# A four-image block on one core: projection with its taps stacked to 128 rows, a shorter split of the scan's rows, and all scans as one sequence beside projections 1 to 3

## The chip, the cores and the metric

The kernel runs on one core of one Trainium2 chip. The metric is device time in microseconds (us) from start to end, the median of several executions. Executions of one kernel on one chip agree within 0.3%. Engines in the profile: PE is TensorE (PEld its weight loads), DVE is VectorE, ACT is ScalarE, POOL is GpSimd, and SPq is the queue from which SyncE issues transfers.

## The reference, cut to what matters

The input is four images of 96 channels and 128 x 128 points. For each image:

```python
z = einsum('bchw,dc->bdhw', x, in_w) + in_b          # x normalised; 96 -> 192 channels
z = silu(depthwise_conv3x3(z, dw_w) + dw_b)           # "projection"
xs = stack([z, z.T, flip(z), flip(z.T)])              # 4 directions, 16384 points each
x_dbl = einsum('bkdl,ked->bkel', xs, x_proj_weight)   # 8 rows: 6 for delta, B, C
delta = softplus(einsum(dts_r, dt_projs_weight) + bias)
dA = exp(delta * A);  dBu = delta * B * xs
h[l] = dA[l] * h[l-1] + dBu[l]                        # the scan
y = h * C + D * xs                                    # the 4 directions are added up
... normalisation of y, product with out_w            # "norm"
... a second block: attention weights ("maps") from 3x3 convolutions, and their application
```

The second block is not changed. What is in front of it is: the projection, the split of the x_dbl rows into three bf16 pieces, and the order in which scans are run.

## The kernel before

A scan is cut into steps of 128 channels x 1024 points. Two images and six groups of channels make 384 steps. One step touches four engines:

```python
def deltas(n, half):        # TensorE "d": pd = wdt x rows; ScalarE: dl = softplus(pd)
def decays(n):              # ScalarE: dA = exp(A * dl), for two steps
def times_u(n):             # GpSimd: dl = dl * u
def spread(n, q):           # TensorE: pB or pC = row B or C on 128 channels
def times_b(n):             # VectorE: pB = dl * pB
def scan(n):                # VectorE: dA = scan(dA, pB)
def times_c(n):             # VectorE: dl = dA * pC
def into_y(n):              # GpSimd: y = y + dl

for n in range(total):      # the order in which the program is written
    spread(n, 1); scan(n)
    times_u(n + 1)
    if n: into_y(n - 1)
    if n % 2 == 0: deltas(n + 3, 0); deltas(n + 3, 1); decays(n + 2)
    yield 2.6
    times_c(n)
    spread(n + 1, 0); times_b(n + 1)
    if n % 2: deltas(n + 3, 0); deltas(n + 3, 1)
    if n % 2: u_in(n + 3)
    else: rows_in(n + 4)
    yield 2.6
```

The compiler has a scheduler that may move instructions within the bounds of their dependences; the order that it chose is fixed in the compiled program.

```python
def rows_in(n):             # split rows of two steps; one transfer of 60 rows for each image
    xr = p1.tile([KS, 2 * SN], BF16, name="xr", bufs=3)
    for a, img in enumerate(imgs):
        nc.sync.dma_start(xr[a * KI : (a + 1) * KI], xsp[img][k][:, sl])

for j in range(2):          # projection: 2 x 96 channels, 9 taps, 97 rows on the array
    for t in range(KK):
        nc.tensor.matmul(pz, lhsT=weff[:, t, j * C : (j + 1) * C],
            rhs=xs[:, q * R + dh : q * R + dh + R, dw : dw + W],
            start=(t == 0), stop=(t == KK - 1))
        if t % 3 == 2 and t < KK - 1: yield 2.6

drain(projections(0, weff, psl))                    # images 0 and 1, no scans
co_run(projections(1, weff, psl), scans, 0.9)       # images 2 and 3, beside the scans of 0 and 1
drain(scans)
co_run(imgs[0].norm(...), last, 0.8)                # scans of 2 and 3 beside image 0's norm and maps
co_run(imgs[0].attend(psl), last, 1.0)
```

co_run interleaves two programs by the numbers that they yield.

## Time and profile before

| | before |
|---|---|
| median | 9351.4 us (3 runs, 9351.3 to 9352.1) |
| TensorE busy, granted clock | 84% of the span, 0.91 |
| a scan step beside the maps | 7.8 us (1070 us, 137 steps in the compiled order) |
| a scan step's work on GpSimd, ScalarE, VectorE | 5.4, 5.0, 4.8 us |

How to read it: a step needs no engine for more than 5.4 us.

### The profile page before, as it was taken

To read this page: it belongs to the slowest core of one execution; us is meant where nothing else is said; L and a number is where in the kernel's file an instruction comes from. 1 tells how busy PE (TensorE), PEld (TensorE's weight loads), DVE (VectorE), ACT (ScalarE), POOL (GpSimd) and SP (SyncE) were. 2 spreads that over 40 slices of the span, in tenths; PEclk is the share of its full clock that TensorE was granted. 3 is DMA by queue.
4 is the path that set the end of the run, shared out by engine and by line. 5 is a ranking of instruction groups with operands and counts; after the bars stand their busy time and mean duration, and the time that the engine had idled before them with its cause. 6 is when DMAs were issued, how large, how long until landed. Compare 5 with 4: busy or idle time off the path is not lost. (4 is left out here: it accounts for less than half of the span.)

```text
span 9352.3 us, 86318 instructions
## 1 busy us (share of the span) xinstructions
PE 7879.3 (84%) x31732; PEld 4127.8 (44%) x31732; DVE 3474.7 (37%) x3463; ACT 3293.0 (35%) x3977; POOL 2188.9 (23%) x1153
## 2 busy tenths in 40 slices
PE   5993993999399948199999929997999989899997
PEld 1331331333032312066665306565656667467763
DVE  1004004267556448637675343322023331130003
ACT  0004003288378547648674141232111241111111
POOL 1003003267447436338684000000000000000000
PEclk9995996999589968599999969998999999999998
DMA  2115114144633345865555678448376474673237
GB/s 67 43 34 128 39 36 120 57 154 133 153 116 114 120 122 164 174 172 175 168 150 164 183 176 199 133 133 168 94 185 159 117 172 110 151 182 85 73 97 197
DMA packets 832687, 1220.49 MB, mean 131 GB/s; under 512 B 141225, under 2 KB 639906, under 8 KB 819977
## 3 DMA queue, kind: packets, MB, share of 16 engines
q1 hardware_dynamic: 830248, 1214.75, 49.7%
q8 instruction: 252, 4.13, 0.2%
q14 instruction: 171, 1.39, 0.1%
q0 software_dynamic: 2016, 0.22, 0.0%
HBM read 869.16 MB, written 345.01 MB: 130 GB/s over the span
## 5 line engine op out<-in xcount | busy, mean ns | idle before, releaser
L352 PE MATMUL bank<-xs,weff 97*96 97x512 f32 x4608 | 2088.5, 605 | 4.7 <-DVE xs L318 2.6
L352 PEld LDWEIGHTS bank<-xs,weff 97*96 97x96 f32 x4608 | 737.9, 165 | 1235.7 <-issue 1216.5
L577 POOL TENSOR_TENSOR y<-y,dl 128x1024 f32<-128x1024 f32 x384 | 1055.3, 2748 | 816.3 <-DVE dl L571 754.4
L551 POOL TENSOR_TENSOR dl<-dl,u 128x1024 f32<-128x1024 f32 x384 | 1011.3, 2643 | 607.1 <-ACT dA L522 292.1
L983 POOL MEMSET vt<- 96x9 f32 x60 | 6.7, 111 | 3345.1 <-DMA vd<-vt 2648.0
L702 PE MATMUL bank<-y,w_v 128*96 128x384 f32 (+1 forms) x2064 | 714.9, 494 | 76.9 <-DMA y<-x1d 69.8
L702 PE MATMUL bank<-y,w_c 128*96 128x384 f32 (+1 forms) x2064 | 706.0, 488 | 58.7 <-ACT half L945 30.9
L555 DVE TENSOR_TENSOR pB<-dl,pB 128x1024 f32<-128x1024 f32 x384 | 470.3, 1225 | 667.3 <-PE pB L532 360.5
L725 PEld LDWEIGHTS bank<-w_k,y 128*128 128x128 f32 x3360 | 659.6, 261 | 40.4 <-issue 31.1
L725 PEld LDWEIGHTS bank<-w_q,y 128*128 128x128 f32 x3360 | 658.4, 260 | 41.9 <-issue 29.3
L725 PE MATMUL bank<-w_q,y 128*128 128x96 f32 (+2 forms) x3360 | 667.8, 352 | 1.6 <-ACT cc L1003 1.6
L725 PE MATMUL bank<-w_k,y 128*128 128x96 f32 (+2 forms) x3360 | 665.8, 352 | 0.0
L361 ACT ACTIVATE zt<-bank,dwb 96x512 f32<-96x512 f32 x256 | 175.0, 683 | 1355.3 <-PE bank L352 1354.5
L532 PE MATMUL pB<-xr,wbc 60*128 60x512 bf16 (+1 forms) x768 | 270.1, 431 | 416.5 <-DVE dA L568 248.0
L1090 PE MATMUL bank<-v,wat 128*32 128x384 f32 (+1 forms) x6336 | 531.2, 481 | 50.0 <-DMA watr<-watd 33.3
L513 PE MATMUL pd<-xr,wdt 60*128 60x512 bf16 (+1 forms) x768 | 276.6, 428 | 320.2 <-DMA xr<-xsp 270.0
L425 ACT ACTIVATE dl<-pd,dtb 128x512 f32<-128x512 f32 x768 | 491.5, 684 | 123.4 <-PE pd L513 102.6
L425 ACT ACT_TABLE_LOAD x328 | 420.8, 1283 | 311.4 <-PE pd L513 306.5
L532 PEld LDWEIGHTS <-wbc 60*128 60x128 bf16 (+1 forms) x1536 | 127.5, 102 | 909.7 <-issue 323.4
L702 PEld LDWEIGHTS bank<-y,w_v 128*96 128x96 f32 x2064 | 334.8, 165 | 415.0 <-issue 388.3
L571 DVE TENSOR_TENSOR dl<-dA,pC 128x1024 f32<-128x1024 f32 x384 | 466.9, 1216 | 134.7 <-PE pC L532 113.9
L702 PEld LDWEIGHTS bank<-y,w_c 128*96 128x96 f32 x2064 | 331.6, 163 | 383.5 <-issue 345.0
(202 smaller groups left out, 8838.7 us busy)
## 6 DMA issues: line engine op xcount, KB each, us to landing
u<-zb SPq DMA_DIRECT2D x192, 1024.0 KB
xr<-xsp SPq DMA_DIRECT2D x256, 240.0 KB
zb<-zt SPq DMA_DIRECT2D x128, 384.0 KB
yms<-y SPq DMA_DIRECT2D x96, 512.0 KB
yc<-yms SPq DMA_DIRECT2D x128, 384.0 KB
y<-x1d SPq DMA_DIRECT2D x336, 97.0 KB
y<-x2d SPq DMA_DIRECT2D x336, 97.0 KB
v<-vd SPq DMA_DIRECT2D x160, 193.6 KB
```

Of the source, the lines that this page charges most:

```text
L352: nc.tensor.matmul(pz, lhsT=weff[:, t, j * C : (j + 1) * C], rhs=xs[:, q * R + dh : q * R + dh + R, dw : dw + W], start=(t == 0), stop=(t ...
L361: nc.scalar.activation(zt[:, j, :, q * R : (q + 1) * R].rearrange("p b h w -> p h b w"), pz.rearrange("p h (b w) -> p h b w", w=UW), AF.Si ...
L425: nc.scalar.activation(dst, src, AF.Softplus, bias=bias)
L513: nc.tensor.matmul(pd, lhsT=wdt[0 : xr.shape[0], g, k], rhs=xr[:, at : at + CH], start=True, stop=True,)
L532: nc.tensor.matmul(p[:, j : j + CH], lhsT=wbc[0 : xr.shape[0], steps[n][0], q], rhs=xr[:, at + j : at + j + CH], start=True, stop=True,)
L551: nc.gpsimd.tensor_mul(t, t, u_view(n))
L555: nc.vector.tensor_mul(p, live[n]["dl"], p)
L571: nc.vector.tensor_mul(live[n]["dl"], live[n]["dA"], live[n]["C"])
L577: nc.gpsimd.tensor_add(v, v, t.rearrange("p (a b) -> p a b", b=W))
L702: nc.tensor.matmul(pc[:, :n], lhsT=w, rhs=y[:, 0:n, o : o + W], start=(at == 0), stop=(at == len(terms) - 1),)
L725: nc.tensor.matmul(pk[:, k0 * C : k1 * C], lhsT=y[:, kh, sw : sw + 382 : 3], rhs=w.rearrange("p t o -> p (t o)"), start=(i == 0), stop=(i ...
L1090: nc.tensor.matmul(pc[p : p + 32].rearrange("p (a b) -> p a b", b=W), lhsT=(wr if k == 2 else ws[k][:, d])[:, c : c + 32], rhs=y, start=(n ...
```

## The change

Three parts. (1) The projection puts channel-and-tap pieces of 128 rows on the array, so that 7 terms take the place of 9, for 128 output channels; the last 64 channels of two row chunks share the array's columns as two tiles. (2) The split works on two pieces in place of four and stores its rows once, in place of three times; the scan's load rebuilds the three copies, with four transfers per image in place of one. (3) All 384 steps are one sequence that starts beside projection 1.

```diff
-                            nc.tensor.matmul(pz, lhsT=weff[:, t, j * C : (j + 1) * C], ...)   # 9 taps, 2 x 96
+                    terms = [(k, d) for d in range(3) for k in range(2)] + [(2, 0)]
+                        jobs = [(0, 128, 0, q)] if q < 2 else [(0, 64, 128, 0), (64, 128, 128, 1)]
+                            nc.tensor.matmul(pz[p:e]..., lhsT=ws[k][:, d, c : c + e - p], rhs=window(ys[k], at, d, n), ...)
 ...
-            for f in range(4):          # split: rows stored three times
+            for f in range(2):          # stored once, as xdt and xbc
 ...
-                    nc.sync.dma_start(xr[a * KI : (a + 1) * KI], xsp[img][k][:, sl])
+                    src = xdt[img][k % 2, k // 2].rearrange("i r l -> (i r) l")[:, sl]
+                    for w in range(3):
+                        nc.sync.dma_start(xr[at + 18 * w : at + 18 * w + 18], src)
+                    src = xbc[img][k % 2, k // 2].rearrange("i r l -> (i r) l")[:, sl]
+                    nc.sync.dma_start(xr[at + 54 : at + KI], src)
 ...
-        for p in range(npair):
-            scans = ssm_scan(zb[p], xsp[p], yms[p])
-            ... co_run(projections(p + 1, weff, psl), scans, 0.9)
+    last = ssm_scan(zb, xdt, xbc, yms, ready)
+        drain(projections([0], weights, psl))
+        co_run(projections(range(1, NB), weights, psl), last, 1.35)
-    co_run(imgs[0].norm(yms[0][0], psl, "left"), last, 0.8)
-    co_run(imgs[0].attend(psl), last, 1.0)
+    co_run(imgs[0].norm(yms[0][0], psl, "left"), last, 1.0)
+    co_run(imgs[0].attend(psl), last, 0.6)
```

A step's own instructions are the same in both kernels.

## The prediction

> **What bounds the kernel now.** I read the page's first two parts for the regimes, then the costliest groups, then the windows view with one window per stage, then the waits of a few windows. The groups give the main actors:
>
> ```profile
> L352 PE MATMUL bank<-xs,weff 97*96 97x512 f32 x4608 | 2088.5, 605 | 4.7 <-DVE xs L318 2.6
> L577 POOL TENSOR_TENSOR y<-y,dl 128x1024 f32<-128x1024 f32 x384 | 1055.3, 2748 | 816.3 <-DVE dl L571 754.4
> L551 POOL TENSOR_TENSOR dl<-dl,u 128x1024 f32<-128x1024 f32 x384 | 1011.3, 2643 | 607.1 <-ACT dA L522 292.1
> L425 ACT ACT_TABLE_LOAD x328 | 420.8, 1283 | 311.4 <-PE pd L513 306.5
> L522 ACT ACT_TABLE_LOAD x322 | 413.1, 1283 | 5.7
> ```
>
> L352 is the projection: 4608 passes, two for each of 2304 fp32 matmuls. L577 and L551 show 384 scan steps. A step costs GpSimd 2.75 + 2.64 = 5.4 us; VectorE 1.23 + 1.22 + 2.35 (scan) = 4.8 us; ScalarE 2 x 0.684 + 1.146 + 0.28 (first passes) + 650/384 loads x 1.283 = 5.0 us. No engine could do 384 steps in less than about 2070 us; the program spends 750 to 5060 us on them. The windows, cut where the counts of L352, L571 and L763 change, show why (columns: window, length, busy of PE, PEld, DVE, ACT, POOL, then granted clock, DMA share, GB/s):
>
> ```profile
> core 0: us, PE busy (x) PEld busy (x) DVE busy (x) ACT busy (x) POOL busy (x), PEclk, DMA share, GB/s
> 117.00:668.00 551.00, 551.00 (x1256) 193.81 (x1257) 46.70 (x45) 48.59 (x68) 18.16 (x29) 1.00 0.15 42
> 668.00:884.00 216.00, 55.35 (x119) 13.95 (x117) 99.42 (x94) 89.98 (x96) 66.98 (x33) 0.54 0.53 128
> 884.00:1445.00 561.00, 558.74 (x1276) 196.40 (x1277) 55.39 (x51) 48.73 (x69) 26.41 (x33) 0.99 0.15 40
> 1445.00:1680.00 235.00, 79.07 (x169) 20.79 (x168) 136.53 (x112) 102.25 (x107) 121.22 (x45) 0.54 0.52 135
> 1680.00:2335.00 655.00, 644.69 (x1632) 219.27 (x1631) 350.19 (x240) 427.79 (x437) 354.89 (x156) 0.99 0.37 115
> 2335.00:2555.00 220.00, 54.90 (x117) 13.55 (x116) 128.86 (x109) 83.09 (x90) 107.07 (x42) 0.53 0.58 144
> 2555.00:3290.00 735.00, 716.78 (x1726) 225.97 (x1726) 401.12 (x272) 486.98 (x497) 409.91 (x179) 0.96 0.37 119
> 3290.00:3420.00 130.00, 20.73 (x45) 4.91 (x44) 46.15 (x32) 46.74 (x49) 33.84 (x14) 0.52 0.51 113
> 3420.00:3990.00 570.00, 314.18 (x679) 95.74 (x677) 418.00 (x396) 399.44 (x443) 270.38 (x126) 0.70 0.65 165
> 3990.00:5090.00 1100.00, 1060.84 (x4482) 707.03 (x4483) 694.66 (x500) 721.38 (x835) 726.92 (x290) 0.97 0.57 167
> ```
>
> Read in order: projection 0, split, projection 1, split, 2, split, 3, split, normalisation of image 0, its attention maps. The projections and maps are bound by TensorE (97 to 100% busy, clock near 1). The four splits are not: TensorE is a quarter busy and the others half. What follows 5090 us (4262 us) does not contain a changed instruction; it is TensorE's as well.
>
> What holds the splits shows in the waits of the first:
>
> ```profile
> POOL dl L551 <- issue: 169.9, 3, 165.9
> PE pd L513 <- DMA xr<-xsp: 104.8, 4, 84.8
> DVE t L403 <- DMA t<-xrow: 39.3, 1, 39.3
> ACT piece L190 <- DMA t<-xrow: 35.0, 2, 34.7
> ```
>
> The scan waits for split rows, and these for a queue of issues. The timeline of the queue gives: 16 column loads 32 us, 96 stores of the first half to 758 us, 96 of the second to 799 us, only then the next image's 16 statistics loads, and projection 1 at 884. In the second split, GpSimd's memset of xs waits 55.2 us for the stores of the pieces: the next projection reuses the split's memory.
>
> **What the Trainium skill says.** "TensorEngine Tiling (Array Packing)", section Tiling Modes: independent tiles of the array run matmuls in parallel; two for outputs up to 64 columns. The trace has the case of four tiles: 1662 passes of L1090 (mostly 384 columns, 32 outputs) took 140.5 us in the chain, 85 ns each, where L352's rate, 435 ns for 512 columns (below), gives 326 ns for a lone pass of 384. It agrees: four ran in the time of one. "Perfetto Trace Analysis", section Identifying the Most-Contended Engine: matmul busy time is no measure of throughput. It agrees: L352's mean is 605 ns, but 574 passes start in the 250 us from 1000 on, 435 ns each, which I use. "TensorE: Matmul & The Clock Gate", Part 1: after idling the array runs at half clock. Agrees: 0.53 in the splits. "ScalarE: Activation LUTs", section What ACT_TABLE_LOAD costs: 1283 ns and a drain of some 1380 ns. The trace has the 1283 ns, but the next ACTIVATE follows at once, so I charge 1.283.
>
> **The change, part by part.**
>
> *Projection.* Before, an image needs 16 strips x 36 matmuls, plus 4 x 16 of L328, at 2 x 0.435 us: 576 x 0.87 + 64 x 0.87 = 557 us (window 1: 551). After, a strip has 7 terms for each of two chunks of 128 channels, and 7 pairs for the remaining 64 channels of both chunks side by side on the columns: 21 slots. The row product has four matmuls in two concurrent pairs: 2 slots. 16 x 23 x 0.87 = 320 us. The gain is 237 us of TensorE per image. Added per strip: seven copies of about 1 MB within the chip, on the DMA queues. That is about 2.5 MB a strip with loads and stores, 125 GB/s over 20 us; windows here reach 260, so I take it as hidden when alone.
>
> *Split.* 192 stores of 7.9 MB become 24 of 3.1 MB; the scan's reads rebuild the triplicate. Column loads stay at 32 us. Each of two halves: load 4, copy 2, three casts 2, two subtractions 2.4: about 17 us, one after the other as there is one buffer; landing 5. 32 + 34 + 5 = 71 us instead of 120. Then statistics, 84 us before with 15 steps beside them; with 9 I take 70. A gap of 140 to 150 instead of 216 to 235; the last, without statistics, 100 instead of 130.
>
> *One sequence of scans.* I counted steps between markers in TensorE's instruction order of the two built programs, where the order is fixed:
>
> before: 14 in split 0, 0 beside projection 1, 20, 64 beside 2, 20, 74 beside 3, 7, 48 in norm, 137 in maps.
> after: 9 in split 0, 54 beside projection 1, 6, 76 beside 2, 20, 76 beside 3, 13, 50 in norm, 80 in maps.
>
> A step's six matmuls cost TensorE: (645 + 717 - 2 x 557)/138 = 1.8 us beside projections; (1061 - 703)/137 = 2.6 us in maps, where 703 us is an image's 3136 passes of maps at the 224 ns that 8500 to 9000 us shows.
>
> - Start: 117 to 138 us, my estimate: more weight pieces, the border rows made through memory, a stack to copy before the first matmul.
> - Projection 0 alone: 320 (551).
> - Gap: 140 (216).
> - Projection 1: 320 + 54 x 1.8 = 417, at 96%: 435 (561).
> - Gap: 140 (235).
> - Projections 2 and 3: 320 + 76 x 1.8 = 457 on TensorE. ScalarE: the order has 301 table loads in steps 96 to 256, so 76 x (1.37 + 1.15 + 0.28 + 2.41) + 48 x 0.68 + casts = 440. VectorE 76 x 4.8 + 45 = 410, GpSimd 410. Four engines at 88% or more cannot mesh perfectly; I take 525 each (655 and 735).
> - Gaps: 150 and 100 (220, 130).
> - Norm: 570, with the same steps.
> - Maps: 703 + 80 x 2.6 = 911, at 97 to 98%: 930 (1100).
> - The rest: 4262.
>
> Sum: 138 + 320 + 140 + 435 + 140 + 525 + 150 + 525 + 100 + 570 + 930 + 4262 = **8235 us**, 12% less.
>
> **The rivals.** *The pairs do not overlap.* Then 7 more slots a strip: 6.1 x 64 = 390 us of TensorE, of which nearly all lies on the path: about 8600. Against it: L1090. *The stack starves TensorE.* Normalising, copying and multiplying form a chain through GpSimd, VectorE and the in-order DMA queue, where scan loads that wait for buffers stand in front. 5 us late in each of 48 strips is 240 us: 8470. For it: DMA would rise from 115 to some 180 GB/s beside projections (a strip's 2.5 MB and 4.75 steps' 3.1 MB in 31 us). Against: a whole bank group, some 13 us, lies between copy and use. *The other engines become the bound.* GpSimd, ScalarE and VectorE at 7.5 us a step, as slow as the best stage beside projections before, add 2 x 45 us: 8325. In the other direction, 6.3 us a step, which 39 to 40 steps in 4250 to 4500 show, gives 8140. *The gain stays hidden.* If the scans were the only bound, faster projections would change nothing. The windows speak against it: GpSimd is 54 to 66% busy until 5090.
>
> **Range and chances.** Gaps may be off by 30 us each, the two full stages by 60 each, maps and start by 60: together about 150, with more room on the slow side for starvation. 8040 to 8440. Within 2% would need 950 us of the gain to vanish.
>
> **What would show it.** Projection 0 alone at 20 us a strip, with pairs starting within tens of ns; if 26, the overlap failed. Between projections, gaps near 140 us with 24 stores. Projections 2 and 3 at 6.9 us a step, TensorE near 88%; if waits of TensorE for y0, y1 or y2 exceed 50 us in sum, the stack starves it. Maps starting near 3045 and ending near 3975. After that, the same 4262 us within 20; if it is not, I have overlooked something in the tail.

## More of the kernel before

In the page of the kernel before, two lines of the 40 slices (tenths of busy time of TensorE, and its granted clock) show the short dips of the splits and little else, and one group shows VectorE's product with B (columns: busy, mean ns of one; idle time in front of it, what ended most of it) waiting for TensorE more than for GpSimd:

```profile
PE   5993993999399948199999929997999989899997
PEclk9995996999589968599999969998999999999998
L555 DVE TENSOR_TENSOR pB<-dl,pB 128x1024 f32<-128x1024 f32 x384 | 470.3, 1225 | 667.3 <-PE pB L532 360.5
```

## The result, and the profile after

The changed kernel takes 9747.8 us (median of 4 runs, 9738.9 to 9751.1) and the kernel before 9351.7 in the same rounds (9351.3 to 9361.5). The ratio is 1.0419, with a 95% interval of 1.0401 to 1.0437. Ratios here are the mean time of one kernel's runs over that of the other's in the same rounds, so not quite the ratio of the medians. The chips of the five groups of runs below gave the kernel before medians from 9352 to 9408 us, so I compare ratios throughout.

It is **4.2% slower**, where 12% faster was predicted. The same lines of the page after, the slices and the groups of the projection and of the scan:

```profile
PE   5846645566376646528999983998989998999997
PEclk9967777777577767758999996999999999999998
L431 PE MATMUL bank<-y,wp 128*128 128x512 f32 (+3 forms) x3584 | 1357.4, 628 | 37.7 <-DMA y<-y 25.3
L670 POOL TENSOR_TENSOR y<-y,dl 128x1024 f32<-128x1024 f32 x384 | 1060.9, 2763 | 1460.8 <-DVE dl L664 1339.1
L648 DVE TENSOR_TENSOR pB<-dl,pB 128x1024 f32<-128x1024 f32 x384 | 470.7, 1226 | 1687.0 <-POOL dl L644 1413.1
```

After projection 0 TensorE is half idle for 16 slices, and its clock falls to 0.7. The projection itself is as cheap as hoped (1357 us of busy time against 2088), and it waits only 38 us for its stack. What grew are the scan's waits: VectorE's product with B waits 1413 us for GpSimd (before, GpSimd was not its main releaser), and GpSimd's addition waits 1339 us for VectorE (754 before). The windows view of four stages (projection 0, 2, 3, and the maps; columns as in the prediction: window, length, busy of PE, PEld, DVE, ACT, POOL, then clock, DMA share, GB/s):

```profile
100.00:440.00 340.00, 331.66 (x1028) 119.41 (x1028) 29.52 (x40) 38.88 (x54) 2.12 (x29) 1.00 0.47 123
1530.00:2420.00 890.00, 564.17 (x1476) 173.44 (x1476) 388.36 (x259) 434.74 (x452) 402.19 (x182) 0.74 0.40 117
2650.00:3520.00 870.00, 598.26 (x1474) 171.52 (x1476) 386.91 (x259) 418.22 (x438) 416.64 (x182) 0.73 0.39 112
4400.00:5470.00 1070.00, 999.63 (x4092) 666.13 (x4091) 419.73 (x315) 432.42 (x539) 415.45 (x174) 0.94 0.43 121
```

Projection 0 alone takes 340 us, where 320 were predicted. Beside projections 2 and 3 no engine is over 70% busy. That is a loop of waits, and the timeline of the changed kernel shows it (start, duration, engine, line, operation; in brackets the idle time in front and its releaser). One turn, from an addition into y to the next:

```profile
2198.82 2.34 POOL L670 TENSOR_TENSOR y<-y,dl 128x1024 f32<-128x1024 f32 x1 [5.18 <-DVE dl L664]
2201.12 2.34 POOL L644 TENSOR_TENSOR dl<-dl,u 128x1024 f32<-128x1024 f32 x1
2203.49 1.23 DVE L648 TENSOR_TENSOR pB<-dl,pB 128x1024 f32<-128x1024 f32 x1 [4.82 <-POOL dl L644]
2204.82 2.35 DVE L661 TENSOR_TENSOR_SCAN dA<-dA,pB 128x1024 f32<-128x1024 f32 x1
2207.27 1.22 DVE L664 TENSOR_TENSOR dl<-dA,pC 128x1024 f32<-128x1024 f32 x1
2208.64 2.34 POOL L670 TENSOR_TENSOR y<-y,dl 128x1024 f32<-128x1024 f32 x1 [5.18 <-DVE dl L664]
```

The product with u at 2201 waits in GpSimd's queue behind the addition of an earlier step, which waits for VectorE; VectorE then waits for that product. Five instructions in a ring take 9.8 us. Their data do not ask for this ring: by the same timeline ScalarE was through with the product's dl at 2196.3, 4.8 us before the product began. (The product's u came in the same load as that of the step before, whose product ran at 2191.3.) It is the order of GpSimd's queue.

That order can be read from the compiled program without a chip. I counted, at each step's spread of C, how many further steps of deltas TensorE has already issued ("TensorE's lead"), and at each addition into y how many further products with u GpSimd has issued ("GpSimd's lead"), as a mean over the 384 steps. Before: 1.79 and 1.27. After: **0.37 and 0.41**. The order of start times in the traces gives the same numbers. TensorE's order also changed in a second way. Its list, near step 40 of the kernel before and step 180 of the changed one, both beside a projection (d: deltas, B and C: spreads, P: projection matmuls, here with those of the row product; with how many in a row):

```
before  P3 B2 d2 P5 C2 d2 P3 B2 P3 C2 P3 B2 d2 P3 C2 d2 P3 B2 P2 C2 d2 ...
after   C2 P18 d2 B2 C2 P4 d2 P9 B2 C2 d4 B2 C2 B2 C2 d2 B2 C2 d2 P4 B2 P3 C2 P22 d2 ...
```

Before, at most five projection matmuls stand in front of the scan's next in this stretch; after, up to 22. An fp32 matmul is two passes of 435 ns, and a run may hold pairs that go side by side; a run of that kind, timed below, took 17.6 us.

### The profile page after: what moved, and what is told of

Read it like the earlier page. It is cut to its first block, busy times and chain, and to the rows that moved or that the text cites. A ratio compares the mean times of both kernels' runs of the same rounds, so it can differ in the third digit from the quotient of the medians. Undisturbed runs are those within 1.5% of the kernel's fastest.

```text
span 9737.1 us, 85329 instructions
## 1 busy us (share of the span) xinstructions
PE 7348.7 (75%) x30708; PEld 3869.2 (40%) x30708; DVE 3377.1 (35%) x3387; ACT 3159.6 (32%) x3820; POOL 2121.1 (22%) x1161
## 5 line engine op out<-in xcount | busy, mean ns | idle before, releaser
L431 PE MATMUL bank<-y,wp 128*128 128x512 f32 (+3 forms) x3584 | 1357.4, 628 | 37.7 <-DMA y<-y 25.3
L625 PE MATMUL pB<-xr,wbc 60*128 60x512 bf16 (+1 forms) x768 | 325.3, 509 | 1278.7 <-DVE dA L661 641.1
L431 PEld LDWEIGHTS bank<-y,wp 128*128 128x128 f32 (+3 forms) x3584 | 479.3, 172 | 827.4 <-issue 778.5
L504 ACT ACT_TABLE_LOAD x306 | 392.6, 1283 | 820.9 <-PE pd L606 818.1
L606 PE MATMUL pd<-xr,wdt 60*128 60x512 bf16 (+1 forms) x768 | 337.9, 505 | 355.9 <-DMA xr<-xbc 287.8
L1099 DVE BATCH_NORM_STATS2 c2st<-cc 96x6 f32<-96x384 f32 (+1 forms) x172 | 94.8, 552 | 1144.0 <-ACT cc L1098 1143.4
```

What stands on the lines that cost most here:

```text
L431: nc.tensor.matmul(pz[p:e].rearrange("p (h w) -> p h w", w=W), lhsT=ws[k][:, d, c : c + e - p], rhs=window(ys[k], at, d, n), start=(i == 0 ...
L504: nc.scalar.activation(dst, src, AF.Softplus, bias=bias)
L606: nc.tensor.matmul(pd, lhsT=wdt[0 : xr.shape[0], g % 3, k], rhs=xr[:, at : at + CH], start=True, stop=True,)
L625: nc.tensor.matmul(p[:, j : j + CH], lhsT=wbc[0 : xr.shape[0], steps[n][0] % 3, q], rhs=xr[:, at + j : at + j + CH], start=True, stop=True,)
L1099: nc.vector.bn_stats(c2st[:, t * 3 + i], to.rearrange("p h w -> p (h w)"))
```

## The experiments

The table has 17 of the 18 runs; the last, after_old_split_pin_pace, is a repeat and told below. "Leads" are TensorE's and GpSimd's in the compiled order. "Long runs" counts the places where over 15 projection matmuls (in the image stages), or over 20 matmuls of norm and maps, stand between two of the scan's. It does not show their length: in before to before_four_reads_pin_all one of them is (nearly) a whole projection without scans beside it, and in the two before_one_sequence runs one has 351 matmuls and one 333. All kernels pass the comparison with the reference.

| kernel | leads | long runs, projection / norm and maps | ratio to before |
|---|---|---|---|
| before | 1.79, 1.27 | 4 / 4 | 1 |
| before_pin | 1.79, 1.99 | 4 / 4 | 0.9957 |
| before_pin_both | 2.06, 2.01 | 4 / 4 | 0.9931 |
| before_serial | 1.81, 0.48 | 5 / 3 | 1.0427 |
| before_four_reads | 0.76, 0.63 | 4 / 30 | 1.0852 |
| before_four_reads_pin_both | 1.98, 1.98 | 4 / 25 | 1.0397 |
| before_four_reads_pin_all | 1.98, 1.98 | 4 / 1 | 1.0083 |
| before_one_sequence | 1.73, 0.91 | 6 / 5 | 1.0604 |
| before_one_sequence_pin_both | 2.04, 2.02 | 6 / 2 | 1.0246 |
| after | 0.37, 0.41 | 29 / 18 | 1.0419 |
| after_pin | 0.37, 1.99 | 29 / 17 | 1.0212 |
| after_pin_both | 1.99, 1.99 | 42 / 26 | 0.9831 |
| after_pin_runs | 1.99, 1.99 | 1 / 26 | 0.9459 |
| after_pin_all | 1.99, 1.99 | 1 / 2 | 0.9358 |
| after_pin_runs_one_read | 1.99, 1.99 | 4 / 6 | 0.9306 |
| after_old_split | 1.45, 0.92 | 9 / 3 | 0.9704 |
| after_old_split_pin_both | 2.09, 2.05 | 10 / 1 | 0.9345 |
| after_old_split_pin_runs | 2.08, 2.05 | 4 / 2 | 0.9282 |
| after_linear | 1.99, 1.99 | every engine as written | 3.87 |

Half-widths of the 95% intervals are 0.0014 to 0.0018, after_linear's aside.

### GpSimd's order alone: after_pin, before_serial, before_pin, after_linear

Theory A says that the order of the scan in the queues was lost; its first form named GpSimd alone. "Pin" ties the addition to its place in the written order:

```diff
-                nc.gpsimd.tensor_add(v, v, t.rearrange("p (a b) -> p a b", b=W))
+                tc.keep_in_program_order(
+                    nc.gpsimd.tensor_add(v, v, t.rearrange("p (a b) -> p a b", b=W))
+                )
```

before_serial is the converse: the kernel before, written so that GpSimd does two products with u and then two additions, and tied to that.

> The changed kernel with one thing added: GpSimd must issue the addition into y of step n-1 behind the multiplication by u of step n+1, as the program states it, so that two multiplications always stand ahead of an addition (0.4 on average in the changed kernel, 1.3 in the kernel before). Theory A (the scheduler's order on GpSimd makes each step a serial loop of GpSimd, VectorE, GpSimd, about 10 to 11 us): steps fall to 6.3 to 7.5 us, time 8150 to 8500 us. Rival B (rows or u arrive late, because four reads a pair and the stack's copies crowd the DMA queue): the waits turn into waits of GpSimd for DMA, time 9500 us or more.

> The kernel before, with its scan's GpSimd order forced to that of the changed kernel: two multiplications by u, two additions into y, nothing ahead. Nothing else is changed. Theory A: a step cannot be shorter than about 10 us, so the maps stage grows from 1100 to 1370 to 1500 us and the stages beside projections by little; time 9550 to 9850 us. Rival B: the order does not matter, 9300 to 9400 us.

> The kernel before with the same pin as after_pin (lead 2 in place of 1.3 on average). Theory A: TensorE bounds its full stages and the lead was enough, so 0 to 2% faster, 9150 to 9350 us; a larger gain would say that the kernel before lost time to its order as well. Rival B: no difference.

> The changed kernel with every engine and queue in program order, nothing reordered by the scheduler. GpSimd's order in the scan is that of after_pin. Theory A: 8200 to 8800 us, as the scan is the same and other work may wait behind earlier work. Rival B: 9500 us or more.

Measured: after_pin 9607.8 us (before 9408.1), 1.0212; before_serial 9807.1, 1.0427; before_pin 9366.1, 0.9957; after_linear 36407, 3.87. before_serial and before_pin came as theory A expects (before_pin by its share; its time is 16 us over the range given, on a chip where the kernel before takes 9408): shortening GpSimd's lead in the kernel before costs 4.3%, with TensorE's order about as it was (1.81, 5 / 3), and lengthening it gains 0.4%. But after_pin missed theory A's range by over 1000 us. GpSimd's order explains 2% and not the whole. The time is in rival B's range, and a part of B's sign is there too: GpSimd waits 397 us for loads of u, against 167 in the changed kernel. What settles B is the next round. after_linear missed as well. It puts every engine and every transfer in the order as written, and shows only that the written order is not fit for all of them.

The timeline of after_pin shows what took over:

```profile
1813.36 2.35 DVE L656 TENSOR_TENSOR_SCAN dA<-dA,pB 128x1024 f32<-128x1024 f32 x1
1817.08 1.01 PE L625 MATMUL pC<-xr,wbc 120*128 120x512 bf16 x2 [0.29 <-DVE dl L664]
1817.89 1.06 PE L606 MATMUL pd<-xr,wdt 120*128 120x512 bf16 x2
1818.60 1.28 ACT L504 ACT_TABLE_LOAD   x1 [4.55 <-PE pd L606]
1823.70 2.86 POOL L644 TENSOR_TENSOR dl<-dl,u 128x1024 f32<-128x1024 f32 x1 [2.82 <-ACT dA L615]
1826.60 1.23 DVE L648 TENSOR_TENSOR pB<-dl,pB 128x1024 f32<-128x1024 f32 x1 [3.70 <-POOL dl L644]
```

pC needs VectorE to free its buffer, the deltas of a later step stand behind pC in TensorE's queue, ScalarE waits for the deltas, GpSimd for ScalarE and VectorE for GpSimd. That is TensorE's lead of 0.37. So the theory was widened to both engines.

### Both leads, and the split's reads: after_pin_both, before_four_reads, after_old_split, after_old_split_pin_both

The second tie puts the first matmul of each spread behind the deltas that were written before it:

```diff
+                    if j == 0:      # order only, no semaphore between engines
+                        tc.add_manual_dep(mm.ins, last_pd[0].ins.name, NoSync, reason="deltas first")
```

before_four_reads puts one line of the change into the kernel before: the same rows, in four transfers.

```diff
-                    nc.sync.dma_start(xr[a * KI : (a + 1) * KI], xsp[img][k][:, sl])
+                    for lo, hi in ((0, 18), (18, 36), (36, 54), (54, KI)):
+                        nc.sync.dma_start(xr[a * KI + lo : a * KI + hi], xsp[img][k][lo:hi, sl])
```

after_old_split keeps the new projection and the one sequence, and takes the old split with its one read.

> The changed kernel with two ties on its order and no other change: GpSimd's addition into y stays behind the multiplications by u traced before it (as in after_pin), and TensorE's spreads of B and C for a step stay behind the deltas traced before them. TensorE's deltas then run 2.0 steps ahead of the spreads of C (0.4 in the changed kernel and in after_pin, 1.8 before), GpSimd 2.0. Theory A (what was lost is the order of the scan on both engines): the loop through TensorE, ScalarE and GpSimd that after_pin still shows opens, steps take 6.3 to 7.5 us, proj2 and proj3 take 500 to 600 us each, time 8150 to 8600. Rival B (with all scans beside projections, a step can't be below 9 us, because the projections' passes stand in TensorE's queue in front of the scan's, or the clock falls): at most 1% faster than after_pin, 9500 to 9650, with steps still near 10 us beside projections.

> The kernel before with one thing of the change: each load of the scan's split rows is issued as four DMAs of 18, 18, 18 and 6 rows in place of one of 60. Same bytes, same results. In the compiler's order TensorE's lead falls from 1.8 to 0.8 steps and GpSimd's from 1.3 to 0.6, though nothing on those engines was edited. Theory A: slower by 2 to 5%, 9550 to 9800, steps in the maps at 9 us or more where the kernel before has 6.3. Rival C (the reads are hidden, and the number of DMAs in the program matters to nobody): within 1% of before.

> The changed kernel with the old split back (four pieces, rows stored three times, one read of 60 rows per image), new projection and one sequence of scans kept. Leads in the order: TensorE 1.45, GpSimd 0.9. The old split costs some 70 us per image where it is exposed, so about 200 to 280 us more than the predicted 8235. Theory A: 8650 to 9050, clearly faster than before, since most of TensorE's lead is back. Rival B (steps beside projections are slow whatever the order): 9700 to 9950, as the changed kernel or slower.

> after_old_split with both ties of after_pin_both; leads 2.1 and 2.05. Theory A: faster than after_old_split, 8350 to 8750, and 100 to 280 us slower than after_pin_both, which is what the shorter split is worth when the order is right. Rival B: within 1% of after_old_split.

Measured (before 9352.5): after_pin_both 9194.2; before_four_reads 10149.0; after_old_split 9077.1; after_old_split_pin_both 8739.4. Rival B falls: the same work beside the same projections is now faster than the kernel before. (Its reason, projection passes that stand in TensorE's queue in front of the scan's, comes back below, as a matter of order.) Rival C, that the number of reads matters to nobody, falls hard: 8.5%, which is more than was expected of theory A. after_old_split was 30 us over its range and after_old_split_pin_both inside. But after_pin_both missed its range by 590 us, and the old split, expected to be 100 to 280 us slower under the same ties, was 455 us faster. Something of the four reads was not tied yet. The timeline of after_pin_both:

```profile
1619.53 15.35 PE L431 MATMUL bank<-y,wp 128*128 128x512 f32 x49
1634.81 0.60 PE L607 MATMUL pd<-xr,wdt 120*128 120x512 bf16 x2
1635.25 0.59 PE L626 MATMUL pC<-xr,wbc 120*128 120x512 bf16 x2
1635.88 1.22 DVE L673 TENSOR_TENSOR dl<-dA,pC 128x1024 f32<-128x1024 f32 x1 [9.45 <-PE pC L626]
1642.00 2.86 POOL L653 TENSOR_TENSOR dl<-dl,u 128x1024 f32<-128x1024 f32 x1 [8.63 <-issue]
```

A run of 54 projection passes from 1617.3, 17.6 us (the window of this view shows the last 49, 15.4 us; the expectations below, which give 10 to 12 us for 20 to 28 of the list's matmuls, took them for single passes), with the scan's pd and pC behind them, VectorE idle for 9.5 us and GpSimd for 8.6. In the compiled order the ties had even made such runs longer: 42 over 15 matmuls, against 29.

### The length of runs: after_pin_runs, after_old_split_pin_runs, and two parts alone: before_pin_both, before_one_sequence

The third tie puts projection matmuls behind the scan's matmuls that were written before them (order only, by the same means as the second). before_one_sequence is the third part of the change alone, with the old projection and split.

> after_pin_both and one more tie: the projection's passes stay behind the scan's passes traced before them, so TensorE's queue holds the projection in runs of at most 12 passes between two passes of the scan (one first run of 158 apart), as the program was written. In after_pin_both 33 runs of 20 to 28 passes (10 to 12 us) and one of 111 stand in the queue, and its timeline shows VectorE waiting 9.5 us and GpSimd 8.6 us behind one of them. Theory A (order of the queues, now the length of runs): each such run costs the scan some 7 to 9 us, 33 of them 230 to 300 us, and steps beside projections go from 8.3 to 7 us or less: time 8800 to 9000. Rival D (the four reads per step cost time of their own, on the DMA queue, which no order of the engines mends): within 1% of after_pin_both, 9100 to 9280.

> after_old_split_pin_both with the same tie. There long runs were rare already (24% of the passes in runs over 20, 23% with the tie), so Theory A: within 1% of after_old_split_pin_both, 8650 to 8800. If it is 3% faster or more, runs of 10 to 20 passes matter too; if slower, the tie itself costs TensorE.

> The kernel before with both ties of after_pin_both. Leads: TensorE 2.06 (1.79 without), GpSimd 2.01 (1.27). before_pin, with GpSimd's alone, was 0.4% faster. Theory A: 0 to 1.5% faster than before, 9210 to 9350: the order that the compiler found for the kernel before was nearly the best, which is why the change looked like a gain to be added to it.

> One part of the change alone: all scans in one sequence beside projections 1 to 3, with the old projection and the old split. Leads in the order: TensorE 1.73, GpSimd 0.9. By the steps of the prediction with the old stage lengths (projections 551, 655, 694, 694 and a little; gaps 216, 230, 220, 130; norm 570, maps 930, rest 4262) 9230. Theory A: 9200 to 9450, as GpSimd's shorter lead takes back up to 200. Rival B (scans beside projections are slow whatever the order): above 9500.

Measured (before 9368.3): after_pin_runs 8861.3, after_old_split_pin_runs 8694.6, before_pin_both 9305.0: all three inside theory A's ranges, and rival D, at 9100 or more, falls. The kernel before gains 0.7% from two ties, the changed one over 9% from three. before_one_sequence, at 9935.8, missed: 490 us over theory A's range, where rival B had it.

### What was still open: before_one_sequence_pin_both, before_four_reads_pin_both, after_pin_runs_one_read, after_pin_all, before_four_reads_pin_all

> before_one_sequence with both ties. Leads: TensorE 2.04 (1.73 without), GpSimd 2.02 (0.91). Theory A: the loop through GpSimd that its waits show (GpSimd 243 us on VectorE's product with C, VectorE 195 us on GpSimd's product with u, in 800 us beside projections) opens and the time comes to the 9230 of the prediction's stage lengths: 9230 to 9480. Rival E (one sequence beside the projections is slow of itself): 9750 or more.

> before_four_reads with both ties. Leads 1.98 and 1.98 (0.76 and 0.63 without). Theory A: the four reads cost nearly nothing by themselves, time near before_pin_both: 9290 to 9450. Rival G (768 more reads on the one queue of issues, which cost time of their own): 9600 or more.

> after_pin_runs with the 54 rows of deltas of a step pair and image read in one DMA in place of three of 18, from rows that are not the right ones (wrong result on purpose; same bytes, same dependences on the split). Theory A: with the order held the number of reads does not matter: within 1% of after_pin_runs, 8780 to 8930. Rival G (each read costs the queue of issues, and so the rows' arrival): 8660 to 8760, the time of after_old_split_pin_runs.

> Not a test of its own: a second profile of after_old_split_pin_runs beside these runs, to compare on the same chip. Expect 8650 to 8740.

Measured (before 9402.3): before_one_sequence_pin_both 9634.7, between both ranges. The two ties take 3.6% off its time (1.0604 to 1.0246); it is still 3.2% behind before_pin_both (1.0246 against 0.9931). The windows view of this run, projection 2:

```profile
1780.00:2700.00 920.00, 833.26 (x1977) 260.73 (x1977) 600.20 (x398) 651.39 (x676) 647.60 (x265) 0.90 0.41 128
```

By the compiled order 114 steps stand in this stage, 8.1 us each. By the prediction's count TensorE would need 557 + 114 x 1.8 = 762 us. So the stage lasts longer than TensorE's work, its clock is at 0.90, and a step that is moved here costs more than 1.8 us. But it is not a fair trial of one sequence: the pace of 1.35 was set for the shorter projection. In the trace the scans that are ready run out early, and projections 1 and 3 end with 351 and 333 matmuls, 344 and 325 us, with no step beside them. What of the 3.2% is the pace and what the sequence was not separated.

before_four_reads_pin_both, at 9779.3, falls to rival G: the leads are back at 2 and yet 4% are lost. after_pin_runs_one_read, 8750.6, is also rival G's. It reads the 54 rows of deltas in one transfer, from wrong rows, and the comparison does not tell these rows apart. after_old_split_pin_pace is after_old_split_pin_runs, unchanged. It is a single repeat of unknown state, 8749.3 us (9 over what was expected) on a chip where before takes 9402.3, a quotient of 0.931 against 0.928.

Rival G says that each read costs by itself. But the compiled order offered another reading: with four reads, the norm and the maps, which no tie had touched, have 25 and 26 long runs, and with one read 4 to 6. The last two runs tie these matmuls as well and leave the four reads in place:

```diff
+    def matmul_in_order(*a, **kw):
+        mm = nc.tensor.matmul(*a, **kw)
+        if last_scan[0] is not None and kw["start"]:
+            behind(mm, last_scan[0])     # order only
+        return mm
```

> after_pin_runs (four reads, right rows) with one more tie: the first pass of each sum of the normalisation and of the maps stays behind the scan's passes traced before it. Runs over 40 passes vanish (longest 34, once; 27% of passes before). Theory A (the reads cost through the order of TensorE's queue alone): ratio to before 0.925 to 0.937 (some 8680 to 8800), that of after_pin_runs_one_read. Rival G (the reads cost by themselves): ratio 0.942 to 0.950, as after_pin_runs.

> before_four_reads_pin_both with the same tie of normalisation and maps. Runs over 40 passes vanish (longest 21; 30% of passes before). Theory A: ratio 0.99 to 1.01, that of before_pin_both (0.993) or a little above. Rival G: ratio 1.03 or more, as before_four_reads_pin_both (1.040).

Measured (before 9407.6): after_pin_all 8805.6 (0.9358, interval 0.9342 to 0.9373), before_four_reads_pin_all 9483.6 (1.0083, 1.0065 to 1.0101). Both ratios are in theory A's range. The four reads cost the kernel before 8.5%. Ties of order alone take that back to 0.8%; against before_pin_both, which has two of the ties, 1.5% are left (1.0083 against 0.9931), which may be the reads' own. The kernel before with the last tie, which would be the like to compare, was not run. In the changed kernel after_pin_all is 0.5% behind the run with one read (0.9358 against 0.9306). after_pin_all, windows of projection 2 and the maps, and the two groups that waited:

```profile
1320.00:1950.00 630.00, 506.04 (x1519) 162.12 (x1520) 427.18 (x284) 503.55 (x515) 433.75 (x193) 0.90 0.60 173
3530.00:4500.00 970.00, 957.31 (x4101) 662.09 (x4100) 425.23 (x319) 475.34 (x573) 422.06 (x176) 0.99 0.48 134
L697 POOL TENSOR_TENSOR y<-y,dl 128x1024 f32<-128x1024 f32 x384 | 1061.0, 2763 | 257.2 <-DVE dl L690 232.8
L674 DVE TENSOR_TENSOR pB<-dl,pB 128x1024 f32<-128x1024 f32 x384 | 470.3, 1225 | 682.2 <-PE pB L643 518.5
```

Projection 2 takes 630 us in place of 890 and the maps 970 in place of 1070. GpSimd's wait falls from 1461 to 257 us, and VectorE's product with B waits for TensorE again and not for GpSimd. The computing instructions are those of the changed kernel; table loads on ScalarE, which follow from the order, are even more (782 against 708).

What this run waits for is no longer the ring but data: in the stage of the norm (2746 to 3530 us) TensorE's deltas wait 186 us for the scan's rows and GpSimd 180 us for u. So rival B's late loads are real, as what is left when the order is held, and not as the cause of the 4%.

## Why the prediction was wrong

The stages, cut where the projections' and the maps' instructions start and stop (in steps of 10 us), against the prediction's own list:

| us | predicted | before | after | after_pin_all |
|---|---|---|---|---|
| start | 138 | 110 | 100 | 110 |
| projection 0 | 320 | 570 | 340 | 330 |
| gap | 140 | 200 | 190 | 190 |
| projection 1 | 435 | 570 | 720 | 510 |
| gap | 140 | 210 | 180 | 180 |
| projection 2 | 525 | 680 | 890 | 630 |
| gap | 150 | 210 | 230 | 190 |
| projection 3 | 525 | 740 | 870 | 610 |
| last gap and norm | 670 | 720 | 880 | 780 |
| maps | 930 | 1070 | 1070 | 970 |
| rest | 4262 | 4272 | 4267 | 4302 |
| sum | 8235 | 9352 | 9737 | 8802 |

- **The step that failed** is in "One sequence of scans": the stages beside the scans. The working counted steps *between markers* in TensorE's order, charged each 1.8 or 2.6 us of TensorE, set the four engines' sums side by side, and added some 15%: "Four engines at 88% or more cannot mesh perfectly; I take 525 each". (Its sums, 457, 440, 410 and 410 us, are 78 to 87% of 525, or 90 to 100% of TensorE's 457.) It took for granted that the engines would still overlap different steps, as they do before. The compiled order that it counted from already had the answer (leads of 0.37 and 0.41, 29 long runs), but the order *within* a step was not looked at, because the diff does not touch it. Of the 1502 us between prediction and profile, 935 go when the order alone is held (9737 to 8802). Of the 567 that are left, by the table, projections 1 to 3 have 265, the first three gaps 130, the last gap and norm 110.
- **No rival named it.** "The other engines become the bound" came closest, with 7.5 us a step. After, a step takes 11.7 us beside projection 2 (76 in 890 us), with no engine bound. (Its reading that GpSimd is "54 to 66% busy until 5090" holds for the full stages; in the gaps of its own windows GpSimd is 26 to 52% busy.)
- **The projection was right.** 340 us for 320; and the waits for the stack are 38 us, under the 50 that the prediction set as its mark. The pairs of 64 columns overlap: a strip takes 340 / 16 = 21 us, where the prediction gave 20 with overlap and 26 without, and the 448 passes of 64 columns in projection 0 start two by two, at most 10 ns apart. Part by part, with the same two ties, the kernel with the new projection is 8.8% faster (0.9345 against 1.0246), about 840 us, where the working had 4 x 237 = 948 of TensorE's time; but a part of that is the pace, which does not fit the old projection.
- **One sequence was mis-sized** even with the order held. (The 3.2% that it cost with the old projection is no measure of it, as the pace did not fit.) Beside projections the best kernels run up to 14 or 15 steps in 100 us, about 7 us a step. The working's 6.9 was near that. But the mean of a stage is higher: projection 2 of after_pin_all has 80 steps in 630 us, 7.9 each. In projection 1 the order puts all 51 steps in the first 400 us and leaves the last 115 us of the projection (158 matmuls) alone; whether a lower pace there would help was not tried.
- **The split was mis-sized**, as far as the gaps tell: with the order held, 180 to 190 us in place of 140 to 150. SyncE's queue in the first gap of the changed kernel:

```profile
446.44 32.34 SPq L481 DMA_DIRECT2D tcol<-xrow  x16
478.82 1.82 SPq L486 DMA_DIRECT2D t<-xrow  x1
507.16 0.52 SPq L486 DMA_DIRECT2D t<-xrow  x1
545.14 0.96 SPq L558 DMA_DIRECT2D xr<-xbc  x1
```

  The column loads take 32 us, as counted. But the load of the second half is issued only after all stores of the first (507), and the last rows that the scan waits for are asked for at 545: 99 us after the start, where 71 were estimated. With the order tied the new split does not beat the old one at all (0.9358 with four ties against 0.9282 with three), so on this evidence it is worth nothing; what part of that is its four reads is not separated.
- **The tail was right**: 4267 us for 4262.
- The clock is a result and not the cause: it falls to 0.73 where TensorE waits for the scan, and with the order held it is back at 0.90.

What stays open: why the scheduler chose a worse order when a load became four. It was not looked into; shown is only that it did (before_four_reads) and what the orders cost. Open too is what one sequence and the four reads are worth by themselves: no run has one sequence with the old projection at a pace that fits it, and none has the kernel before with all ties. after_old_split_pin_runs (0.9282) is the fastest kernel run, 7% faster than before and 11% faster than the changed kernel.

## What to carry to other kernels

When work of several engines is pipelined by hand, the queue order of each engine is part of the design, and a scheduler may undo it after an edit that touches none of it, such as one more transfer in a load. Before adding up what a change saves, compare in the compiled order how many steps each engine runs ahead, and how long the other work's runs are between two of the chain's instructions; if they shrank or grew, tie the order and measure again before judging the change. In a trace the sign is a stage in which no engine is near full, the clock is low, and a small ring of instructions each waits for the one before.

## What the Trainium skill lacked or had wrong

- Trainium skill, "Perfetto Trace Analysis", Identifying the Most-Contended Engine and Optimization Strategy, starts from the busiest engine of a regime. Here the stages beside projections 1 to 3, which have 730 of the 935 us, have no engine near its bound (PE 63%, ACT 49%, POOL 45%, DVE 44% of projection 2 after). The sections go on to what the gaps of the one engine wait for, which here leads around a ring; no page says to compare the orders of the engines' queues.
- Trainium skill, "TensorE: Matmul & The Clock Gate", Part 1 (on engine queue depths) says that ScalarE, VectorE and GpSimd take their queues strictly in order, and Part 3 says the same of matmuls. The traces agree: a product with u whose inputs were ready at 2196.3 waited behind an addition until 2201.1. But no page says to check the order that a scheduler has chosen, or what it can cost: 4.3% from GpSimd's order alone (before_serial), 8.5% from one load split in four (before_four_reads), 10.2% between two orders of the same changed kernel (0.9358 against 1.0419).
- Trainium skill, "ScalarE: Activation LUTs", What ACT_TABLE_LOAD costs, adds a drain of some 1380 ns to the 1283 ns of the load. In the traces the load has 1283 ns, and no drain stands before or after it: in the changed kernel an ACTIVATE ends at 2202.81, the load runs from 2202.82 for 1.28 us, and the next ACTIVATE starts at 2204.12.
